# First lora products of both pairs of a batch issued together, and a new order of all steps

## The chip, the core and the metric

The kernel runs on one core of a Trainium2 chip. The metric is device time in microseconds. Before the change three runs took 446.77, 448.08 and 449.16, a median of 448.08. Within a core five queues work beside each other: TensorE (PE; its weight loads are shown as PEld), VectorE (DVE), ScalarE (ACT), GpSimd (POOL) and SyncE (SP), the last of which only issues DMAs here. Each takes its own instructions strictly in the order in which the program lists them, and waits on semaphores for the results of others.

## What is computed

The input `x` has 64 samples of 64 channels and 1024 positions. A grouped convolution (4 groups, 9 taps) with a bias per channel and a conditioning term per sample gives `v`; `v` goes through a linear layer of 1024 x 1024 with a low-rank (lora) term that is chosen per batch element by a gate, and the result is added to `x`.

```python
v   = conv1d(x, weight, groups=4, pad=4) + (cond_128 @ c_weight.T)[:, :, None] + fside[None, :, None]
A_b = sum_n gate[b, n] * lora_A[n]          # 32 x 1024
B_b = sum_n gate[b, n] * lora_B[n]          # 1024 x 32
out = x + v @ kernel + bias
        + (v @ A_b.T) @ B_b.T               # batch b: 8 samples of x
        + (v @ A_shared.T) @ B_shared.T
```

There are 8 batch elements. All is fp32; the kernel splits each operand of a large product into a high and a low part (`..hi` rounds on ScalarE, `..lo` subtracts on VectorE or GpSimd) and adds three products, high by high, high by low and low by high.

## The kernel before, in words

The 64 samples are worked in 16 **pairs** p = 0 to 15 of four samples each, and a batch element b has the two pairs 2b and 2b+1. A pair goes through these steps; the number after a step's name is the pair, then the group, quarter or product, and a last letter v, p or a says on which engine a step is put that could run on several.

- `xload p g` (L293) brings one of the four channel groups in on SP's queue. From pair 3 on, the convolution is done on sums and differences: `xdiff` (L326), `xohi`, `xolo`, `xdhi`, `xdlo` split it, `convo` (3 matmuls of 256 columns, into PSUM tile cm) and `convd` (6 of them, into cv) multiply (L346). `evmid` adds the conditioning to cm, with four activations on ScalarE (L364) or one addition on VectorE (L366); `evac` (L378) adds the two and writes `v`; `turned` (L387) transposes it into `z` on VectorE. Pairs 0 to 2 use the plain form `xhi`, `xlo`, `conv`.
- The linear layer is a 2 x 2 block product with seven products in place of eight. `asum` (L412, GpSimd) makes sums of quarters of z, `yhi` and `ylo` split the left operand, `prod p j` (L592) is product j, 12 matmuls of 512 columns. `keep` (ScalarE, L636), `xsum`, `ysum`, `radd`, `yadd` and `total` (VectorE, some on GpSimd) put the products together with the residual, which `rload` (SP) brings in; `store` (ScalarE's queue) writes the result. Pair 0 uses `plain p b k`, without the seven-product form.
- The lora term has two products. `lora p` (L602) is the first, z by A_b: 16 fp32 matmuls with 32 columns of weights, 32 records in the profile. It reads all four groups of the pair's z. Then `axlow` (ScalarE), `axsum` (VectorE), `axhi` (ScalarE) and `axlo` (VectorE) add and split its result, and `delta p b` (L660), one matmul each, adds the second product into the accumulators of quarter b. A_b and B_b come from `lload`, `mix` (TensorE, L528), `mixout`, `mixput`, `aload`, `bload`, `bhi` and `blo`.
- At the start the weights are loaded (`wload`), completed with the shared lora term (`fmm` on TensorE, `fadd` on VectorE), summed (`wsum`) and split (`whi`, `wlo`). `gmask` makes a small matrix out of the gate; `twsum`, `thi` and `tlo` prepare the convolution's weights; `cwide`, `cmul` and `csum` make the conditioning table.

What sets the order is a list: the string `ORDER` (L50 to L245) names every step once, and the program walks through it and emits each step's instructions. The instructions of each engine are then tied to each other in exactly that order, so nothing is moved by a scheduler. Tiles come from pools with fixed numbers of buffers (5 for products in PSUM, 2 for convolutions in PSUM, 4 for z, y, r and c), so that a step also waits until the tile it writes is free.

Before the change every pair had its own `lora` step at a place of its own, for instance `lora 2` between `bload 1 0` and `axlow 2` on L96 and `lora 3` on L100; `lora 0` and `lora 1` stood close together on L79.

Of the kernel before, what the change touches and what calls it, by code (L numbers as in the profile page):

```python
# [22 lines left out]
BP = NP // NB  # L23
# [27 lines left out]
small 1, warm, twload 1, busy 29, twload 0, cwload, gload, ctload, cwide, cmul, thi 2, small 0, thi 0, tlo 0 v,  # L51
xload 0 0, xhi 0 0, tlo 2 p, xload 0 1, xlo 0 0 v, conv 0 0, twsum v, xhi 0 1, xlo 0 1 v, conv 0 1, sbload 1,
sbhi 1, csum, evac 0 0 v, turned 0 0, xload 0 2, xhi 0 2, xload 0 3, saload 0, sblo 1 p, xlo 0 2 p, evac 0 1 v,
turned 0 1, saload 1, gmask, xhi 0 3, conv 0 2, xlo 0 3 p, sahi 1, conv 0 3, sahi 0, salo 0 v, fmm 0 1,
sbload 0, sbhi 0, fmm 1 1, wload 1 0, evac 0 2 a, xload 1 0, sblo 0 v, fmm 1 0, salo 1 v, xload 1 1, xhi 1 0,
xhi 1 1, xlo 1 1 p, xlo 1 0 v, turned 0 2, yhi 0 0, ylo 0 0 p, wload 0 1, fadd 0 1, evac 0 3 a, fadd 1 0,
conv 1 0, whi 7 0, fmm 4 0, turned 0 3, xload 1 2, xhi 1 2, wlo 7 0 v, fmm 3 0, wload 1 1, conv 1 1, fadd 1 1,
wload 4 0, fmm 0 0, whi 0 1, wload 0 0, fadd 0 0, evac 1 0 a, plain 0 1 0, fadd 4 0, xlo 1 2 p, turned 1 0,
whi 0 0, wlo 0 1 p, fmm 2 1, fmm 2 0, yhi 0 7, evac 1 1 a, conv 1 2, fmm 5 0, wload 2 1, wload 2 0, fadd 2 0,
wlo 0 0 p, plain 0 0 0, xload 1 3, fadd 2 1, wload 5 0, xhi 1 3, fmm 4 1, xlo 1 3 p, plain 0 0 1, whi 0 2,  # L60
ylo 0 7 v, fadd 5 0, plain 0 3 0, whi 7 1, yhi 0 4, wload 3 0, fadd 3 0, whi 0 3, wload 5 1, fmm 3 1, conv 1 3,
turned 1 1, wlo 7 1 v, wload 3 1, xload 2 0, plain 0 1 1, fadd 3 1, whi 7 2, evac 1 2 v, wlo 7 2 p, wload 4 1,
wlo 0 3 p, wlo 0 2 v, lload 0 6, plain 0 2 0, whi 7 3, plain 0 3 1, fadd 4 1, wload 7 1, turned 1 2, whi 1 1,
plain 0 1 2, lload 0 7, xhi 2 0, plain 0 0 2, ylo 0 4 v, plain 0 3 2, xlo 2 0 v, plain 0 2 1, fmm 5 1,
evac 1 3 a, xload 3 0, wlo 7 3 v, plain 0 2 2, turned 1 3, whi 1 0, yhi 0 1, ylo 0 1 v, fadd 5 1, whi 6 1,
conv 2 0, wload 7 0, thi 1, xdiff 3 0 0 v, wload 6 0, evac 2 0 a, lload 1 5, wlo 1 0 p, fmm 7 0, fadd 7 0,
plain 0 2 3, plain 0 0 3, fmm 6 0, lload 0 2, plain 0 3 3, plain 0 1 3, fadd 6 0, lload 0 5, whi 6 0, asum 1 2,
yhi 1 2, lload 0 0, yhi 1 0, plain 0 0 4, plain 0 2 4, wsum 2 2 v, whi 2 2, lload 1 1, wlo 1 1 p, plain 0 0 5,
fmm 6 1, tlo 1 v, plain 0 2 5, rload 0 2, wlo 6 0 v, wsum 2 1 v, wsum 2 3 v, whi 1 2, wlo 1 2 v, plain 0 1 4,
whi 2 1, asum 1 3, whi 1 3, wlo 1 3 p, xload 2 2, wload 6 1, fadd 6 1, xload 2 1, whi 6 2, lload 0 1, xhi 2 2,  # L70
plain 0 3 4, lload 0 4, plain 0 2 6, lload 1 0, lload 0 3, wsum 2 0 v, fmm 7 1, plain 0 2 7, xload 2 3,
plain 0 0 6, fadd 7 1, whi 6 3, total 0 2, lload 1 6, mix 0 0, mixout 0 0 a, wlo 6 2 v, xhi 2 1, wlo 6 3 v,
wlo 6 1 v, wsum 3 2 v, xlo 2 2 v, mix 0 3, mixout 0 3 a, mix 0 2, mixout 0 2 a, wsum 3 0 v, wsum 5 0 v,
mixput 0 0, whi 2 3, mix 0 1, wsum 3 1 v, mix 1 0, mixput 0 3, mixout 0 1 a, xdiff 3 0 1 p, wsum 4 0 v,
conv 2 2, wlo 2 2 v, whi 2 0, wlo 2 0 v, ylo 1 2 v, plain 0 1 5, wsum 5 1 v, rload 0 0, wsum 5 2 v, wsum 4 2 v,
xlo 2 1 v, plain 0 0 7, mixput 0 1, ylo 1 0 p, mixput 0 2, wlo 2 1 v, prod 1 0, plain 0 1 6, wsum 3 3 v,
wsum 5 3 v, rload 0 1, plain 0 3 5, wsum 4 3 v, bihi, whi 3 2, keep 1 0, plain 0 1 7, lload 1 3, wsum 4 1 v,
plain 0 3 6, mixout 1 0 a, lload 1 7, mix 1 3, aload 0, whi 5 3, yhi 1 3, rload 0 3, lload 1 2, ylo 1 3 v,
mixout 1 3 a, total 0 1, lora 0, mix 1 1, turned 2 0, lora 1, whi 5 0, bilo, xohi 3 0, lload 1 4, mix 1 2,  # L79
whi 4 2, wlo 4 2 v, mixout 1 1 a, xolo 3 0 v, whi 3 0, wlo 3 0 v, wlo 3 2 v, yhi 1 1, ylo 1 1 v, mixout 1 2 a,  # L80
asum 1 5, total 0 0, whi 4 1, conv 2 1, axlow 1, axsum 1, xload 3 2, wlo 4 1 p, wlo 2 3 v, whi 4 0,
plain 0 3 7, axlow 0, axsum 0, mixput 1 0, mixput 1 3, wlo 4 0 v, xhi 2 3, xlo 2 3 v, wlo 5 3 v, axhi 1,
prod 1 1, biput 0, axlo 1, whi 3 3, asum 1 6, yhi 1 6, wlo 3 3 v, mixput 1 1, evac 2 1 a, turned 2 1, aload 1,
mixput 1 2, total 0 3, evac 2 2 v, turned 2 2, bload 0 0, whi 3 1, axhi 0, prod 1 2, keep 1 2, conv 2 3,
bhi 0 0, biput 1, yhi 2 0, evac 2 3 a, blo 0 0 v, axlo 0, yhi 1 4, bload 0 1, wlo 3 1 p, prod 1 3, ylo 2 0 v,
delta 0 0 1, total 0 0 1, bhi 0 1, blo 0 1 v, ylo 1 6 p, prod 1 6, whi 4 3, delta 0 3 1, wlo 4 3 v, store 0 0,
ylo 1 4 p, turned 2 3, delta 0 2 1, total 0 3 1, xdhi 3 0, convo 3 0, yhi 1 5, whi 5 1, ylo 1 5 v, xdlo 3 0 v,
delta 1 0, total 0 2 1, xload 3 1, keep 1 3, prod 1 4, evmid 3 0 a, store 0 3, xohi 3 1, xdiff 3 1 0 v,
xdiff 3 1 1 p, wlo 5 1 p, delta 0 1 1, total 0 1 1, wlo 5 0 v, xolo 3 1 p, convd 3 0, evac 3 0, turned 3 0,
asum 2 3, rload 1 0, convo 3 1, yhi 2 1, xdhi 3 1, xdlo 3 1 v, prod 2 0, whi 5 2, store 0 2, delta 1 2,  # L90
xload 3 3, keep 2 0, wlo 5 2 p, yhi 2 3, prod 1 5, total 1 0, xohi 3 3, xolo 3 3 v, asum 2 2, xdiff 3 2 0 p,
store 1 0, convo 3 3, evmid 3 1 a, xdiff 3 2 1 p, convd 3 1, ylo 2 3 v, prod 2 3, rload 1 3, delta 1 1,
ylo 2 1 v, xsum 1, asum 2 5, prod 2 1, xdhi 3 2, evac 3 1, turned 3 1, rload 1 2, radd 1 2 v, xdlo 3 2 v,
xdiff 3 3 0 v, delta 1 3, xohi 3 2, xdiff 3 3 1 p, yhi 2 5, xolo 3 2 v, ylo 2 5 p, yhi 2 2, ylo 2 2 v,
evmid 3 3 a, radd 1 3 v, convo 3 2, total 1 2, store 0 1, evmid 3 2 a, convd 3 2, xdhi 3 3, xdlo 3 3 v,
rload 1 1, radd 1 1 v, bload 1 0, lora 2, axlow 2, asum 2 6, prod 2 2, total 1 1, convd 3 3, evac 3 2,  # L96
turned 3 2, axsum 2, xload 4 0, xohi 4 0, xolo 4 0 p, bhi 1 0, yhi 2 4, ylo 2 4 v, axhi 2, prod 2 5, keep 2 3,
yhi 3 0, ysum 1 p, xdiff 4 0 0 v, xdiff 4 0 1 v, prod 2 4, store 1 1, xload 4 1, xohi 4 1, xolo 4 1 p,
yadd 1 v, blo 1 0 v, xdhi 4 0, axlo 2, delta 2 0, yhi 2 6, evac 3 3, keep 2 2, xdlo 4 0 v, convo 4 0,
turned 3 3, convd 4 0, rload 2 0, evmid 4 0 a, total 1 3, total 2 0, ylo 3 0 v, lora 3, xdiff 4 1 0 v,  # L100
xdiff 4 1 1 p, asum 3 3, yhi 3 3, prod 3 0, convo 4 1, ylo 3 3 v, evac 4 0, turned 4 0, xdhi 4 1, xload 4 3,
xohi 4 3, xdlo 4 1 v, asum 3 2, xolo 4 3 v, yhi 3 2, ylo 2 6 v, xload 4 2, xdiff 4 2 0 p, store 1 2,
xdiff 4 2 1 p, xohi 4 2, prod 3 3, yhi 3 1, bload 1 1, evmid 4 1 a, delta 2 2, ylo 3 2 v, xolo 4 2 v, asum 3 5,
store 2 0, convd 4 1, xdhi 4 2, xsum 2, convo 4 2, evmid 4 2 a, evac 4 1, xdlo 4 2 v, rload 2 2, radd 2 2 p,
total 2 2, xdiff 4 3 0 v, xdiff 4 3 1 p, prod 2 6, turned 4 1, yhi 3 4, bhi 1 1, convd 4 2, evac 4 2, keep 3 0,
prod 3 2, ylo 3 1 v, rload 2 3, radd 2 3 v, ysum 2 v, convo 4 3, yadd 2 v, xdhi 4 3, xdlo 4 3 v, ylo 3 4 v,
aload 2, prod 3 1, convd 4 3, turned 4 2, blo 1 1 p, xload 5 0, yhi 3 5, xohi 5 0, keep 3 2, asum 3 6,
keep 3 3, xload 5 1, xohi 5 1, delta 2 3, prod 3 4, delta 2 1, xdiff 5 0 0 p, xdiff 5 0 1 v, axlow 3,
ylo 3 5 p, evmid 4 3 a, total 2 3, prod 3 5, store 2 3, xolo 5 0 p, rload 2 1, yhi 3 6, radd 2 1 p, rload 3 0,
axsum 3, evac 4 3, axhi 3, turned 4 3, yhi 4 0, axlo 3, delta 3 0, xload 5 2, xdhi 5 0, store 1 3, xdlo 5 0 v,  # L110
convd 5 0, convo 5 0, ylo 3 6 v, bload 2 0, ylo 4 0 v, xdiff 5 1 0 v, xdiff 5 1 1 p, total 2 1, prod 3 6,
evmid 5 0 a, prod 4 0, asum 4 3, yhi 4 3, evac 5 0, xsum 3, yhi 4 4, ylo 4 3 p, delta 3 3, delta 3 2,
total 3 0, ylo 4 4 v, lora 4, xolo 5 1 p, xdhi 5 1, xdlo 5 1 v, store 3 0, yhi 4 1, ylo 4 1 v, xohi 5 2,
convo 5 1, keep 4 0, bhi 2 0, prod 4 1, rload 3 3, asum 4 2, yhi 4 2, radd 3 3 v, turned 5 0, xdiff 5 2 0 p,
ysum 3 v, evmid 5 1 a, xdiff 5 2 1 v, ylo 4 2 v, delta 3 1, xolo 5 2 p, rload 3 1, radd 3 1 p, blo 2 0 v,
# [702 lines left out]
```

## Time and profile before

| what | before |
| --- | --- |
| median of three runs | 448.08 us |
| the execution with profile | 447.48 us |
| span of its instructions | 445.7 us |
| first lora blocks (`lora`) | 16, of which 14 stand alone |
| evictions of cm (`evmid`) on ScalarE | 52, 48.2 us of records |
| share of the span, by the chain that ended last | TensorE 91%, DMA 4%, VectorE 2% |

The page has a line of busy time for each engine, and the same in 40 slices; the chain of work that ended last; and the costliest groups of instructions. Queries of the trace give the waits by engine and releaser (time in total, times, longest), timelines of an engine (start, duration, line, operation, output and inputs) and sums of busy time by stretch of the span. A record's duration is longer than the step from one start to the next where instructions are pipelined. TensorE's clock was granted in full throughout.

### The profile page before, as it was taken

The numbers are of one execution on the slowest core, as the hardware profiler recorded it, in microseconds if no ns is written. First come the engines' busy times: TensorE is split into PE (matmuls) and PEld (weight loads), VectorE is DVE, ScalarE is ACT, GpSimd is POOL, SyncE is SP. The second block draws the span as 40 slices with busy tenths as digits, with TensorE's granted clock in tenths as the row PEclk, the third lists the DMA queues.
The fourth block names the chain that finished last, engine by engine and source line by source line (L and its number), as shares of the span: only waits on it lengthen the run. The fifth ranks groups of instructions, "written<-read, shape, count | busy, mean of one in ns | idle before, by whom it ended". The sixth has DMA issues, their size and how long they took to land.

```text
span 445.7 us, 7717 instructions
## 1 busy us (share of the span) xinstructions
PE 438.3 (98%) x2557; PEld 358.7 (80%) x2557; DVE 391.3 (88%) x615; ACT 251.2 (56%) x639; POOL 234.5 (53%) x202
## 2 busy tenths in 40 slices
PE   8999999999999999999999999999999999999996
PEld 7677658888888888888878888888888888888884
DVE  5998979899899899889899899899798989887783
ACT  5877468556655566446555655646554745654440
POOL 3766024754747653555444445464656475467543
PEclk9999999999999999999999999999999999999999
DMA  8999582461625463534345453443536354262243
GB/s 229 300 280 308 147 251 66 142 186 49 186 82 158 136 190 110 170 120 136 97 139 147 151 182 91 119 142 90 175 98 186 95 169 151 72 222 90 91 150 118
DMA packets 52488, 67.05 MB, mean 150 GB/s; under 512 B 6112, under 2 KB 34016, under 8 KB 52448
## 3 DMA queue, kind: packets, MB, share of 16 engines
q1 hardware_dynamic: 42512, 49.83, 38.9%
q10 hardware_dynamic: 9936, 16.73, 10.2%
q8 instruction: 20, 0.33, 0.3%
q14 instruction: 20, 0.16, 0.1%
HBM read 47.65 MB, written 18.87 MB: 149 GB/s over the span
## 4 chain that ended last, share of the span: by engine, by line
PE 91%; DMA 4%; DVE 2%; issue 1%; SPq 0%; ACT 0%; ACTq 0%; DVEq 0%
PE mm_a L592 19%; PE mm_d L592 18%; PE mm_c L592 17%; PE mm_b L592 9%; PE cv L346 8%; PE cm L346 4%; PE axp L602 3%; PE cv L318 2%; DMA wr<-in_dram 2%; PE mx L528 2%; PE mm_a L580 1%; PE mm_c L580 1%; DMA ls<-in_dram 1%; DMA ctt<-in_dram 1%; PE mm_d L580 1%; PE mm_a L660 1%
## 5 line engine op out<-in xcount | busy, mean ns | idle before, releaser
L592 PE MATMUL mm_a<-wh,y 128*128 128x512 f32 x240 | 79.6, 392 | 0.0
L592 PE MATMUL mm_d<-wh,y 128*128 128x512 f32 x240 | 79.2, 391 | 0.0
L592 PE MATMUL mm_c<-wh,y 128*128 128x512 f32 x240 | 79.1, 391 | 0.0
L364 ACT ACTIVATE md<-cm,cadd 128x64 f32<-128x64 f32 x208 | 48.2, 315 | 44.8 <-PE cm L346 41.1
L326 POOL TENSOR_TENSOR xf<-xt 128x256 f32<-128x256 f32 x45 | 33.3, 747 | 49.4 <-DVE xd L270 39.4
L265 ACT CAST xd<-xf 128x512 fp32r<-128x512 f32 x52 | 32.5, 626 | 44.9 <-PE cv L346 20.7
L265 ACT CAST y<-s 128x512 fp32r<-128x512 f32 x60 | 37.2, 624 | 30.5 <-POOL s L412 15.3
L592 PEld LDWEIGHTS mm_a<-wh,y 128*128 128x128 f32 x240 | 45.1, 188 | 9.9 <-issue 0.4
L592 PEld LDWEIGHTS mm_d<-wh,y 128*128 128x128 f32 x240 | 45.1, 188 | 9.2 <-issue 0.2
L592 PEld LDWEIGHTS mm_c<-wh,y 128*128 128x128 f32 x240 | 45.1, 188 | 9.1 <-ACT c L636 0.2
L387 DVE STREAM_TRANSPOSE z<-v 128x512 f32<-128x512 f32 x64 | 45.4, 709 | 3.2 <-PE axp L602 1.9
L592 PE MATMUL mm_a<-wl,y 128*128 128x512 f32 x120 | 46.9, 391 | 0.0
L592 PE MATMUL mm_c<-wl,y 128*128 128x512 f32 x120 | 46.8, 390 | 0.0
L592 PE MATMUL mm_d<-wl,y 128*128 128x512 f32 x120 | 46.8, 390 | 0.0
L346 PE MATMUL cv<-xd,th 128*128 128x256 f32 x208 | 45.7, 282 | 0.4 <-DVE xd L270 0.4
L378 DVE TENSOR_TENSOR v<-cv,md 128x512 f32<-128x512 f32 x52 | 35.7, 686 | 7.7 <-PE cv L346 2.5
L270 DVE TENSOR_TENSOR xd<-xf,xd 128x512 fp32r<-128x512 f32 x41 | 34.5, 842 | 7.6 <-ACT xd L265 7.4
L270 DVE TENSOR_TENSOR y<-s,y 128x512 fp32r<-128x512 f32 x49 | 38.2, 782 | 3.0 <-ACT y L265 2.7
L592 PE MATMUL mm_b<-wh,y 128*128 128x512 f32 x120 | 39.6, 391 | 0.0
L346 PEld LDWEIGHTS cv<-xd,th 128*128 128x128 f32 x208 | 35.5, 188 | 2.4 <-DVE xd L270 0.6
L265 ACT CAST y<-z 128x512 fp32r<-128x512 f32 x49 | 30.6, 625 | 11.8 <-DVE c L641 4.5
L326 DVE TENSOR_TENSOR xf<-xt 128x256 f32<-128x256 f32 x59 | 33.7, 587 | 0.2
(132 smaller groups left out, 1008.2 us busy)
## 6 DMA issues: line engine op xcount, KB each, us to landing
xt<-in_dram SPq DMA_DIRECT2D x64, 258.0 KB, 3.2
r<-in_dram SPq DMA_DIRECT2D x64, 256.0 KB, 3.5
out_dram<-r ACTq DMA_DIRECT2D x63, 256.0 KB, 2.6
ls<-in_dram SPq DMA_DIRECT2D x16, 256.0 KB, 4.6
br<-eff SPq DMA_DIRECT2D x48, 64.0 KB, 2.8
wr<-in_dram SPq DMA_DIRECT2D x16, 176.0 KB, 4.2
eff<-ls SPq DMA_DIRECT2D x16, 128.0 KB, 2.7
wr<-in_dram SPq DMA_DIRECT2D x16, 80.0 KB, 3.9
```

The lines of the kernel that those rows point to most:

```text
L265: nc.scalar.copy(dst, src)
L270: engs[eng].tensor_tensor(dst, src, f32(hi), ALU.subtract)
L318: nc.tensor.matmul(ps, a[:, 2 * kt, g, :], b[:, :, kt:kt + P], start=(n == 0), stop=(n == 5))
L326: engs[eng].tensor_tensor(xdf[p, g][:, e], m, odd(p, g), ALU.subtract)
L346: nc.tensor.matmul(ps, a[:, w, g, :], b, start=(n == 0), stop=(n == 2))
L364: nc.scalar.activation(t[:, n], cpm[p, g][:, n], ACTF.Identity, bias=c[:, n:n + 1])
L378: nc.vector.tensor_tensor(v.rearrange("p n (i e) -> p e n i", e=2), cps.pop((p, g)), mid.pop((p, g)).unsqueeze(1).to_broadcast([P, 2, 4, H ...
L387: nc.vector.transpose(z[:, :, :, :, gg, :], vs.pop((p, g)).rearrange("p m j -> p (m j)"))
L528: nc.tensor.matmul(mps[w, j][n * e:n * e + n], gm.rearrange("p b i -> p (b i)"), lraw[w, 2 * j + e], start=True, stop=True)
L580: nc.tensor.matmul(acc[p, BLOCKS[b]], m[:, kk, :], n, start=(k == 0 and q == 0), stop=(k == 7 and q == 2))
L592: nc.tensor.matmul(ps, a[:, k, :], b[bb, k], start=s, stop=(k == HK - 1 and q == 2), skip_group_check=not first)
L602: nc.tensor.matmul(axp[q * R:q * R + R, p % 2, :], a[:, k, :], zs[p, hf][:, k, :], start=k < 2, stop=k >= 6)
```

## The change

A new step `loras b` issues the first lora products of both pairs of a batch, one behind the other. It takes the place of the single `lora` steps for batches 1 to 7; batch 0 keeps `lora 0` and `lora 1`. The whole string `ORDER` is replaced by another order of the same steps, from the first line to the last, with new choices of engine for many of them. No step's code is altered.

```diff
+    def loras(b):
+        for p in range(BP * b, BP * b + BP):
+            lora(p)
```

The start of the list, which is typical of the rest:

```diff
-small 1, warm, twload 1, busy 29, twload 0, cwload, gload, ctload, cwide, cmul, thi 2, small 0, thi 0, tlo 0 v,
-xload 0 0, xhi 0 0, tlo 2 p, xload 0 1, xlo 0 0 v, conv 0 0, twsum v, xhi 0 1, xlo 0 1 v, conv 0 1, sbload 1,
+cwload, warm, busy 29, twload 1, gload, gmask, ctload, twload 0, twsum v, xload 0 0, cwide, saload 0, thi 2,
+xload 0 1, thi 0, tlo 2 v, small 0, tlo 0 p, xhi 0 0, xlo 0 0 v, sahi 0, salo 0 v, sbload 0, xhi 0 1,
+xlo 0 1 v, sbhi 0, sbload 1, sbhi 1, cmul, sblo 0 v, csum, conv 0 0, evac 0 0 v, turned 0 0, xload 0 3,
...
-rload 1 1, radd 1 1 v, bload 1 0, lora 2, axlow 2, asum 2 6, prod 2 2, total 1 1, convd 3 3, evac 3 2,
-turned 3 3, convd 4 0, rload 2 0, evmid 4 0 a, total 1 3, total 2 0, ylo 3 0 v, lora 3, xdiff 4 1 0 v,
...
+ylo 2 5 v, yhi 3 0, xdhi 4 0, ylo 3 0 v, xdlo 4 0 v, loras 1, rload 1 3, radd 1 3 v, yhi 2 6, convo 4 0,
...
+prod 15 0, keep 15 0, evac 15 3, turned 15 3, loras 7, yhi 15 4, rload 14 2, prod 14 6, radd 14 2 p, ysum 14 p,
...
+prod 15 4, delta 15 1, rload 15 2, total 15 0, store 15 0, radd 15 2 p, delta 15 2, total 15 2, store 15 2,
+prod 15 6, rload 15 1, radd 15 1 v, totalh 15 1 1, storeh 15 1 1, totalh 15 1 0, storeh 15 1 0
```

How the steps with a choice of engine are placed before and after, where the numbers differ by two or more (the rest moves by one, or trades places pair by pair):

| step | before | after |
| --- | --- | --- |
| `evmid` | ScalarE 52 | ScalarE 36, VectorE 16 |
| `blo` | VectorE 10, GpSimd 6 | VectorE 13, GpSimd 3 |
| `xdlo` | VectorE 41, GpSimd 11 | VectorE 38, GpSimd 14 |
| `xlo` | VectorE 7, GpSimd 5 | VectorE 10, GpSimd 2 |
| `xolo` | VectorE 30, GpSimd 22 | VectorE 28, GpSimd 24 |
| `wlo` | VectorE 21, GpSimd 11 | VectorE 23, GpSimd 9 |
| `wsum` | VectorE 16 | VectorE 14, GpSimd 2 |
| `radd` | VectorE 36, GpSimd 9 | VectorE 38, GpSimd 7 |
| `ysum` | VectorE 13, GpSimd 2 | VectorE 11, GpSimd 4 |

On TensorE the mixes are placed differently too: before, `mix 0 0`, `0 3`, `0 2`, `0 1` and `1 0` stand in one row; after, `mix 0 0` and `mix 0 2` each stand alone between `plain` steps, and `mix 0 3`, `1 0`, `0 1` and `1 2` stand in one row.

## The prediction, made before the changed kernel ran

> **What bounds the kernel now.** The views were read in this order: the page's busy time, the waits of TensorE, the sums by stretch, then TensorE's and VectorE's timelines. One execution with profile took 447.48 us, of which 445.7 are the span; the median of the three runs shown is 448.08, 0.6 above it. Sums below are made against the 447.48 and 0.6 is added at the end.
>
> ```profile
> PE 438.3 (98%) x2557; PEld 358.7 (80%) x2557; DVE 391.3 (88%) x615; ACT 251.2 (56%) x639; POOL 234.5 (53%) x202
> ```
>
> TensorE is busy all but 7.4 us. Of its waits, all that the view names come to 3.2 us, and those that are not the warm-up or a `conv` of the first pairs are these:
>
> ```profile
> PE cv L346 <- DVE xd L270: 0.4, 1, 0.4
> PE mx L528 <- DMA ls<-in_dram: 0.4, 1, 0.4
> ```
>
> So the total is TensorE's list of work plus what it loses early. The sums by stretch (busy us and counts of PE, PEld, DVE, ACT, POOL; clock; DMA share) tell who is next:
>
> ```profile
> 20.00:45.00 25.00, 25.00 (x108) 19.33 (x108) 23.71 (x37) 17.87 (x40) 16.73 (x13) 1.00 0.95 293
> 45.00:70.00 25.00, 24.55 (x157) 15.04 (x154) 21.91 (x39) 15.97 (x35) 4.27 (x3) 1.00 0.65 180
> 70.00:100.00 30.00, 29.99 (x172) 24.86 (x171) 26.96 (x39) 18.62 (x51) 18.14 (x15) 1.00 0.47 144
> 100.00:130.00 30.00, 30.00 (x180) 25.40 (x179) 28.25 (x46) 17.12 (x46) 17.84 (x17) 1.00 0.33 99
> ```
>
> The reader is to see that VectorE is at 88 to 95% beside TensorE from 20 to 130 us, ScalarE and GpSimd are far below, and the DMA engines are nearly full until 45. VectorE is the engine that can become the bound.
>
> **The lora blocks.** A lora block is 32 matmul records (16 matmuls in two passes) with weights of 32 columns. Its edges on TensorE's timeline (start, duration):
>
> ```profile
> 140.41 0.40 PE L660 MATMUL mm_b<-bst,axt 98*128 98x512 f32 x1
> 140.65 0.39 PE L660 MATMUL mm_c<-bst,axt 98*128 98x512 f32 x1
> 140.97 1.08 PE L602 MATMUL axp<-z,ar 128*32 128x128 f32 x32
> 141.98 0.39 PE L346 MATMUL cm<-xo,th 128*128 128x256 f32 x1
> 142.21 0.28 PE L346 MATMUL cm<-xo,tl 128*128 128x256 f32 x1
> 142.32 0.28 PE L346 MATMUL cm<-xo,th 128*128 128x256 f32 x1
> ```
>
> From start to start, a 512-wide matmul takes 0.23 to 0.24 but the last one before the block takes 0.32: 0.09 to get in. The block takes 1.01. The first 256-wide matmul after it takes 0.23 where the next takes 0.11: 0.11 to get out. All 14 blocks of pairs 2 to 15 show the same 0.09 and 0.11 within 0.01, so an edge pair costs **0.20**. Merging two blocks removes one exit and one entry; the seam inside is a step like those within the block, 0.03 on average. Seven merges: 7 x 0.20 = 1.4 off. Against it, the new order puts `mix 0 0` and `mix 0 2` alone between `plain` steps, where before five mixes stood together; a mix block shows 0.32 on entry too, and I take 0.20 each: 0.4 on. Net **-1.0**. Ends: 0 (if the seam costs what the edges cost) and -1.4.
>
> Here the Trainium skill speaks against the change. "TensorE: Matmul & The Clock Gate", section "Step-by-step: what each phase is for", says weight loads are pulled ahead of matmuls in flight, so the next tile's weights load while this one runs. By that rule a block's edge costs nothing and the merge is worth 0. In the trace the first weight load of the block starts only with the block, at 140.97, after 0.36 us idle. I take the row: -1.0, not 0.
>
> **VectorE's running sum.** The order is one list of steps, and each engine takes its own in that order. So for each TensorE step I add what VectorE has in its queue up to the result that this step needs, and compare it with TensorE's own sum up to there. Records of VectorE overlap, so I use start-to-start steps:
>
> ```profile
> 6.21 0.68 DVE L270 TENSOR_TENSOR tl<-tw,th 128x512 fp32r<-128x512 f32 x1
> ...
> 6.81 0.69 DVE L270 TENSOR_TENSOR xsl<-xt,xsh 128x516 fp32r<-128x516 f32 x1
> ...
> 8.62 0.41 DVE L736 TENSOR_TENSOR cadd<-pc,fst 128x256 f32<-128x256 f32 x1
> ```
>
> 0.60 is such a step when undisturbed; means over the execution (some steps take 1.3) are: z 0.65, v 0.67, y 0.74, xd 0.76, r<-r,c 0.69, xo 0.57, xf 0.49, wl 0.65, wr 0.60 to 0.64, sums out of PSUM 0.61. TensorE: product 2.745, plain 0.68, conv 1.42, convd 0.71, convo 0.355, delta 0.235, mix 0.45, lora 1.21. VectorE starts at 4.8 (`cwide`), TensorE's real work is set at 7.4, the first `conv`.
>
> Before, the worst place is `conv 2 3`, which needs the PSUM tile that `evac 2 2` frees. TensorE: 7.4 + 11 conv 15.6 + 32 plain 21.8 + 16 fmm 3.8 + 8 mix 3.6 + 3 products 8.2 + 2 lora 2.4 + cmul 0.9 = 63.8. VectorE: 4.8 + 62.2 for 97 steps = 67.0. TensorE must lose **3.2** there, whatever happens. From 75 us on VectorE is ahead (by 1.3 at 82, 5.9 at 123, 9 at 145), and this is why no wait is left later.
>
> After, the worst place is `convo 3 2`, behind `evac 3 1`: TensorE 7.4 + 75.1 = 82.5; VectorE 4.8 + 82.4 (127 steps) = 87.2, a deficit of **4.7**. It is 3.7 at 120 (`delta 2 3` behind `blo 1 1`), 1.4 at 123, 0.9 still at 167 (`prod 5 5` behind `ylo 5 5`), and VectorE is ahead only from 180 on. Two causes. Up to `evac 3 1` it has six more steps (121 before: 3 more xlo, 2 more wlo, 2 more ylo, ...) while two products fewer stand ahead on TensorE. And 16 `evmid` move from ScalarE to VectorE: on ScalarE four activations each, 48.2 / 52 = 0.93; on VectorE nearest is the row of cadd above, same size and also out of PSUM, 0.41 recorded, 0.36 a step: 16 x 0.36 = 5.8 more on VectorE, 2.2 of it (six) before 167; where VectorE is ahead it costs 0. With all other moves between v, p and a its whole sum grows by about 7 (388 to 395). ScalarE's relief and GpSimd's nearly equal load (238 to 236) are worth nothing, since nobody waits for them for long.
>
> The start is part of this sum, not added to it: `gmask` (1.25) and `twsum` (0.61) now stand ahead of `cwide`, so the first `conv` moves from 7.5 to about 9.3. `gmask` waits for gg, second of ScalarE's DMAs instead of third, so not later than `cwide` waited before. Before, TensorE lost 0.78 and 0.54 to xsl soon after; those are absorbed. Loads: weights that `fadd` needs land by my count of bytes (0.28 MB/us) up to 3 us behind TensorE's new order at 20 us, but VectorE gets to those fadd 3 to 4 us later still, so it hides them. Later moves of xload, rload, store and bload past each other on SP: before, SP blocks up to 10 us on a store and nobody waits; cost 0, at most 1 to 2 if an xload is caught behind a late store. A new wait: `loras` needs the z tiles of both pairs, and all four z buffers are held until then; the next `turned` on VectorE is queued at least one product later, so 0. If that cover went, evac, xdiff and with them `convd` would stand behind it.
>
> The end: `prod 15 5` needs `ylo 15 5`, now on GpSimd behind `radd 14 2` 1.35, `ysum 14` 1.34, two `asum` 1.5 each, plus `yhi` 0.62 and itself 1.38: 7.7 after `turned 15 3`, which itself ends 1 to 1.5 after `convd 15 3`. TensorE has `prod 15 0`, `loras 7`, `prod 14 6` and up to four deltas before it, 2.7 + 2.2 + 2.7 + 0.9 = 8.5. I take 0, at most 1. `rload 15 1` and `radd 15 1` stand behind the last product in the list, but nothing on SP holds the load back: 0, at most one radd, 0.7.
>
> **Sum.** Edges -1.0. Deficit 4.7 instead of 3.2: +1.5. While VectorE sets the pace, its own short waits (for ScalarE mostly) count: it idled 3.0 of 70:100, of which I take a third, +1.0. The one mid-run loss before, 0.6 at 233, need not come back: -0.6. Together +0.9: 448.4 in that execution's terms, **449.0** against the median.
>
> **Rivals.**
> Slower: VectorE stays the pace far beyond 87 us. Its idle time of before then counts in full: to 123, 3.7 + 3.0 + 1.4 - 3.2 = 4.9, less 1.0, is +3.9, **452.0**; to 168, 0.9 + 8.0 - 3.2 - 1.0 = +4.7, 452.8. It decides once VectorE's idle time between 67 and 123 is over 3. For it: almost no lead until 167. Against: before, much of that idle time was VectorE waiting for TensorE, which falls away.
> Faster: VectorE's backlog removes its waits. Before it lost 1.9 near 57 us, a `turned` waiting for a `lora` that waited for its DMA; here VectorE gets there later. -1.0 + 1.5 - 1.9 - 0.9 = -2.3, **445.8**. Against: it asks for everything at once.
> No effect of the merge itself: +1.9, 450.0; against it are the equal 0.09 and 0.11 of 14 blocks.
>
> **How the numbers follow.** Likeliest case 0.50 (447 to 450.3, no-effect included), slower rival 0.39, faster 0.11. About 0.5%, or 2.2 us, is what a measurement of this kernel can tell from no change. So faster 0.11, same 0.50, slower 0.39. The range 446 to 453.5 leaves out the faster rival's tail and the slower one's.
>
> **What would show it.** 7 blocks of 64 records with one entry of 0.09 and one exit of 0.11; cm evictions of about 0.41 on VectorE; VectorE at 95% or more from 20 to 120; TensorE waits on VectorE between 20 and 110, none after 180. Wrong if TensorE waits after 180, or if waits on DMA or GpSimd carry the loss.

## The result, and the profile after

The change made the kernel slower: 459.83 us (459.67 to 460.67, 4 runs) against 448.30 (446.77 to 449.16, 4 runs), a ratio of **1.0265** with a 95% interval of 1.0234 to 1.0296. The forecast was 449.0 with a range up to 453.5: the measured time lies 6.3 us above its upper end. The profiled execution took 460.67, with a span of 458.8 against 445.7.

The page of the changed kernel, its busy time, the granted clock in 40 slices and the chain that ended last, and below it the chain of the kernel before:

```profile
PE 445.5 (97%) x2557; PEld 361.1 (79%) x2557; DVE 403.1 (88%) x633; ACT 236.5 (52%) x574; POOL 236.8 (52%) x201
...
PEclk9999999999899999999999999999999999999999
...
PE 75%; DVE 10%; DMA 6%; issue 3%; ACT 2%; SPq 1%; POOL 1%; DVEq 0%; ACTq 0%; POOLq 0%
```
```profile
PE 91%; DMA 4%; DVE 2%; issue 1%; SPq 0%; ACT 0%; ACTq 0%; DVEq 0%
```

Three things are to be seen. TensorE is busy for 7.2 us more than before although it does the same 2557 instructions. One slice of the clock, near 115 us, is an 8. And TensorE's part of the chain went from 91% to 75%, VectorE's from 2% to 10%.

What TensorE waited for (in total, times, longest):

```profile
PE cm L345 <- DVE v L377: 2.3, 1, 2.3
PE idle L704 <- DVE axt L698: 1.2, 1, 1.2
PE pf L474 <- POOL sa L269: 1.1, 1, 1.1
PE pf L474 <- POOL sb L269: 1.0, 1, 1.0
PE mm_a L663 <- DVE axt L626: 1.0, 1, 1.0
PE cv L345 <- DVE xd L269: 0.9, 1, 0.9
PE cm L345 <- DVE xo L269: 0.6, 1, 0.6
```

The second is the warm-up, which was there before. The pf lines are two `fmm` of the start, which wait from 12 and from 19 us on. The other four are new, and each is a single long wait: `delta 2 0` and `convo 4 2` near 112 us, `convo 8 2` at 230, `convd 10 3` at 291. The sums by stretch, in the columns used before:

```profile
20.00:45.00 25.00, 24.67 (x103) 18.67 (x104) 23.50 (x38) 17.40 (x41) 13.32 (x9) 1.00 0.98 303
45.00:70.00 25.00, 25.00 (x161) 15.48 (x160) 23.19 (x38) 15.62 (x37) 6.68 (x6) 1.00 0.61 167
70.00:100.00 30.00, 30.00 (x147) 24.99 (x146) 27.36 (x42) 19.34 (x50) 16.38 (x15) 1.00 0.45 142
100.00:130.00 30.00, 28.46 (x185) 22.92 (x184) 27.52 (x48) 13.64 (x35) 11.29 (x10) 0.94 0.43 132
```

From 45 to 100 us TensorE has no gap. In the last row it idles for 1.54 us, and its clock is 0.94 there. How the halved clock looks, on TensorE's timeline of that place (start, duration):

```profile
111.68 0.40 PE L591 MATMUL mm_b<-wh,y 128*128 128x512 f32 x1
113.05 0.47 PE L663 MATMUL mm_a<-bst,axt 98*128 98x512 f32 x1 [0.98 <-DVE axt L626]
113.51 0.36 PE L345 MATMUL cm<-xo,th 128*128 128x256 f32 x1
113.70 0.28 PE L345 MATMUL cm<-xo,tl 128*128 128x256 f32 x1
114.54 0.64 PE L345 MATMUL cm<-xo,th 128*128 128x256 f32 x2 [0.56 <-DVE xo L269]
114.98 0.41 PE L345 MATMUL cm<-xo,tl 128*128 128x256 f32 x1
115.19 0.41 PE L345 MATMUL cm<-xo,th 128*128 128x256 f32 x1
115.41 0.63 PE L591 MATMUL mm_a<-wh,y 128*128 128x512 f32 x1
115.83 0.63 PE L591 MATMUL mm_a<-wl,y 128*128 128x512 f32 x1
```

The 256-wide steps take 0.21 instead of 0.12 and the 512-wide ones 0.42 instead of 0.23. The clock's own record has 0.5 for 3.41 us from 114.74 on. In 3.4 us at such steps, 3.4 x (1 - 0.234 / 0.42) = 1.5 us of TensorE's work is lost in this execution, on top of the waits that stand right before (from start to start, 1.15 and 0.72 above a normal step). In time it is less. Of the four executions two had a mean granted clock of 0.996 (460.67 and 459.89 us) and two of 1.000, with no such stretch (459.67 and 459.77): 0.1 to 1.0 us apart. Why the rest of the 1.5 does not show was not tried.

To add up the loss, each step of TensorE (the time from one instruction's start to the next one's) was set against a normal one for its shape (512 columns 227 ns, 256 columns 117, a record of a lora block 31.6). The normal steps sum to some 425 us in every kernel here. What is above them, in us by stretch, with the two kernels of the experiments that matter most beside it (`a_lay` is the changed order at the old addresses, `a_fix4` the same with its lists mended):

```
stretch (us)   before   after   a_lay   a_fix4
  0 -  40        5.6     8.0     7.9     7.9
 40 - 100        2.9     2.0     1.4     1.4
100 - 140        0.5     4.7     3.2     3.6
140 - 220        1.5     2.3     1.1     1.3
220 - 300        2.0     6.1     6.8     2.5
300 - end        2.5     4.8     1.9     1.8
sum             15.0    27.9    22.2    18.5
```

The column of after is higher even from 300 us on, where TensorE has only one wait of 0.4. There every product is a little slower: its 512-wide step is 234.1 ns on average (1263 steps, the few over 300 left out) where it was 228.4, the same in every stretch of 40 us. 1263 x 5.7 ns is **7.2 us**, the largest single part of the loss, and nothing in the diff seemed to touch it.

### The profile page after: what moved, and what is told of

Same layout as the page of the kernel before. It is cut to its first block, busy times and chain, and to the rows that moved or that the text cites. A ratio compares the mean times of both kernels' runs of the same rounds, so it can differ in the third digit from the quotient of the medians.

```text
span 458.8 us, 7648 instructions
## 1 busy us (share of the span) xinstructions
PE 445.5 (97%) x2557; PEld 361.1 (79%) x2557; DVE 403.1 (88%) x633; ACT 236.5 (52%) x574; POOL 236.8 (52%) x201
## 4 chain that ended last, share of the span: by engine, by line
PE 75%; DVE 10%; DMA 6%; issue 3%; ACT 2%; SPq 1%; POOL 1%; DVEq 0%; ACTq 0%; POOLq 0%
PE mm_d L591 16%; PE mm_c L591 16%; PE mm_a L591 14%; PE mm_b L591 8%; PE cv L345 7%; PE cm L345 3%; PE axp L601 2%; DMA wr<-in_dram 2%; DVE y L269 2%; PE mx L527 1%; DVE r L669 1%; DMA xt<-in_dram 1%; DVE xd L269 1%; DMA sbr<-in_dram 1%; DVE r L652 1%
## 5 line engine op out<-in xcount | busy, mean ns | idle before, releaser
L591 PE MATMUL mm_a<-wh,y 128*128 128x512 f32 x240 | 81.5, 401 | 0.0
L591 PE MATMUL mm_d<-wh,y 128*128 128x512 f32 x240 | 80.5, 397 | 0.0
L591 PE MATMUL mm_c<-wh,y 128*128 128x512 f32 x240 | 80.4, 396 | 0.0
L363 ACT ACTIVATE md<-cm,cadd 128x64 f32<-128x64 f32 x144 | 33.2, 316 | 41.0 <-PE cm L345 36.5
L591 PE MATMUL mm_a<-wl,y 128*128 128x512 f32 x120 | 48.1, 401 | 0.0
L269 DVE TENSOR_TENSOR y<-z,y 128x512 fp32r<-128x512 f32 x42 | 36.3, 869 | 1.7 <-ACT y L264 1.6
L269 DVE TENSOR_TENSOR xd<-xf,xd 128x512 fp32r<-128x512 f32 x38 | 31.2, 822 | 6.2 <-ACT xd L264 6.2
L269 POOL TENSOR_TENSOR xd<-xf,xd 128x512 fp32r<-128x512 f32 x14 | 20.4, 1456 | 30.9 <-ACT xd L264 30.9
```

The lines of the kernel that those rows point to most:

```text
L269: engs[eng].tensor_tensor(dst, src, f32(hi), ALU.subtract)
L363: nc.scalar.activation(t[:, n], cpm[p, g][:, n], ACTF.Identity, bias=c[:, n:n + 1])
L591: nc.tensor.matmul(ps, a[:, k, :], b[bb, k], start=s, stop=(k == HK - 1 and q == 2), skip_group_check=not first)
```

## The experiments

The theories at first: **layout**, that new addresses of tiles in SBUF make the matmuls slower; **order**, that the new lists do (VectorE's load, other engines' traffic). Each kernel below was timed beside the kernel before on the same chip, and its ratio to that is given with a 95% interval.

### Is it the addresses?

The pool gives places in the order in which kinds of tiles are first named. Before, `xhi 0 0` and `xhi 0 1` claimed the places of xo and xd, and then `sbload 1` the 57 weight pieces. After, `saload 0` comes ahead of both. Addresses stand in no trace. Read off the compiled kernels, the pieces start at byte 69440 of a partition before and at 61152 after, the y tiles at 204608 in both; the 8288 bytes between are the size of the two xo tiles (2080 each) and the xd tile (4128) that changed places with the pieces. Two kernels moved the pieces by 32 bytes, the changed one (`a_align`) and the one before (`b_shift`), with the same edit:

```diff
     def piece(name, shape=(P, HN), dtype=F32):
-        return work.tile(list(shape), dtype, tag="w", name=name, bufs=57)
+        if not pads:
+            pads.append(work.tile([P, 8], F32, tag="pa", name="pa", bufs=1))
+        t = work.tile(list(shape), dtype, tag="w", name=name, bufs=57)
+        if len(pads) < 2:
+            pads.append(work.tile([P, 8], F32, tag="pb", name="pb", bufs=1))
+        return t
+    pads = []
```

> The changed kernel with two unused 32-byte tiles, one ahead of the 57 weight pieces in SBUF and one behind them, so that the pieces begin at a multiple of 64 bytes as they did before (the change's new first step to claim a piece, a load of the shared lora, had put them 32 bytes beside it), and all other tiles keep their place within 64 bytes. Theory LAYOUT: the 512-wide matmuls that stream a weight piece take 234 ns a step after and 227 before (means 234.4 and 228.7) because of the 32 bytes; about 1347 of them x 5.7 ns = 7.7, so 459.8 - 7.7 = 452.1 us, and the median step is 227 again. Rival ORDER: the longer step comes from the new order (queues, semaphores, what VectorE and GpSimd do at the same time), so 459.8 us and a step of 234.

> The kernel before with the same two 32-byte tiles, which here put its weight pieces 32 bytes beside a multiple of 64; its order is untouched. Theory LAYOUT: 448.3 + 7.7 = 456.0 us, median step of the products 234. Rival ORDER: 448.3 us, step 227.

`a_align` took 457.99 (1.0194, 1.0169 to 1.0219) with a mean step of 232.5; `b_shift` 454.15 (1.0119, 1.0094 to 1.0144) with 233.0. Its order untouched, the kernel before lost 5.3 us to unused bytes: layout matters. But `a_align` did not get its step back, so alignment to 64 bytes isn't the rule. The next two kernels exchanged the whole layout:

```diff
# a_lay: the changed kernel, places of xo and xd claimed first
     def piece(name, shape=(P, HN), dtype=F32):
+        if not room:
+            for n in range(2):
+                room.append(work.tile([P, 4, JB], F32R, tag="xo", name=f"room{n}", bufs=2))
+            room.append(work.tile([P, 2, 4, JB], F32R, tag="xd", name="room2", bufs=1))
# b_lay: the kernel before, a step "room" ahead of xhi 0 0
+    def room():
+        for n in range(57):
+            piece(f"room{n}")
```

> The changed kernel with every tile at the SBUF address that it had before (the places of xo and xd are claimed ahead of the first weight piece); order untouched. Shifting by 32 bytes both ways moved the mean step of a product's matmul between four values, one for each layout (228.4 before, 233.0 shifted; 234.1 after, 232.5 aligned to 64), so it is the layout but not the 64 bytes alone. Theory LAYOUT: the mean step is 228.4, 1263 x (234.1 - 228.4) = 7.2 less, 459.8 - 7.2 = 452.6 us, or some 2 less where the clock is not halved. Rival CONTENTION (the engines' traffic of the new order makes the step longer and the address only shifts it a little): step 231 or more, 456 us or more.

> The kernel before with every tile at the address that it has in the changed kernel; order untouched. Theory LAYOUT: mean step 234.1, 1261 x 5.7 ns = 7.2 more, 455.5 us. Rival CONTENTION: 228.4 to 231, at most 451.5.

`a_lay`: step 228.4, 455.29 us (1.0153, 1.0133 to 1.0173). `b_lay`: step 234.1, 455.02 (1.0137, 1.0120 to 1.0154). The steps are exactly the forecast ones. The groups by line show the same thing in the recorded duration (busy us, mean ns). Before, then after, `a_lay` and `b_lay`:

```profile
L592 PE MATMUL mm_a<-wh,y 128*128 128x512 f32 x240 | 79.6, 392 | 0.0
```
```profile
L591 PE MATMUL mm_a<-wh,y 128*128 128x512 f32 x240 | 81.5, 401 | 0.0
```
```profile
L597 PE MATMUL mm_a<-wh,y 128*128 128x512 f32 x240 | 79.4, 391 | 0.0
```
```profile
L594 PE MATMUL mm_a<-wh,y 128*128 128x512 f32 x240 | 80.9, 398 | 0.0
```

The same order is slower or quicker by its addresses alone. In time it is 4.5 us (459.83 to 455.29) on the changed kernel and 6.6 (448.44 to 455.02) on the one before, less than 7.2 on the first; that TensorE's waits take up part of it where VectorE sets the pace fits, but was not tried by itself. Rival contention fell: with the new order and all its traffic the step is 228.4.

What of the addresses is it? Five more kernels are the one before with other sums of unused bytes ahead of the pieces, each run once (`[P, 8]` above becomes another size, and the tile behind fills up to 256):

> The kernel before with its weight pieces 64 bytes further (64 and 192 unused bytes ahead of them and behind them), all others in place within 256 bytes. A look at the step alone. If it depends on the piece's start within 128 bytes (64 of 128: 228.4; 0: 232.5; 32 or 96: 233 to 234), it is 232.5 here. If it is 64 bytes that count and the rest came from the other tiles, it is 228.4.

> As b_w64, with the pieces 128 bytes further. If the start within 128 bytes counts, the mean step is 228.4 again; if it is the distance between the piece and the y tile (0 of 256 before), it is higher, 232 to 233.

> The kernel before with its weight pieces 32 bytes further and all other tiles in place within 256 bytes: a piece starts 32 bytes (of 256) behind a y tile. If the distance of the two operands sets the step, this is a value of its own, between those at 0 (228.4) and 64 (229.7) or above both; if 32 of 64 bytes is what costs, 233 to 234.

> As b_d32 at a distance of 96. By distance: between 64 (229.7) and 128 (232.5), near 231; by 32 of 64 bytes: 233 to 234.

> As b_d32 at a distance of 192, the pieces at a multiple of 2048. By distance: between 160 (234.1) and 224 (233.0), near 233.5; by the piece's own start: 0 of 256 should be at least as good as 64 of 256, 228.4 or less.

All layouts, by the distance from a y tile (the weights of the matmul) to a weight piece (what it streams), within 256 bytes:

```
distance   mean step (ns), kernels               piece's own start
   0       228.4  before, a_lay and its repairs       64
  32       233.2  b_d32                               96
  64       229.7  b_w64                              128
  96       233.5  b_d96                              160
 128       232.5  a_align; 232.6 b_w128             0; 192
 160       234.1  after, b_lay                       224
 192       233.2  b_d192                               0
 224       233.0  b_shift                             96
```

The one pair with equal distance and different starts, `a_align` and `b_w128`, has the same mean and the same distribution of steps (most at 228 to 233, a fifth at 236 to 241). The pair with the same start 0, `a_align` and `b_d192`, has different ones (in `b_d192` most are at 231 to 237). So the step goes with the distance of the two operands and not with the piece's own start, as far as these two pairs tell. It doesn't grow with the distance: my 231 for 96 was a miss, 0 is best, 64 costs 1.3 ns, all others 4 to 6. Tiles that moved along with y (z, v, xf) aren't told apart from it; but the matmul reads only these two. The single times of the five (452.40 to 456.76 us) are all above the median of before.

### What is a merge worth?

The edges of a merged block, on the timeline of the changed kernel (x64 is the whole block):

```profile
216.67 0.28 PE L345 MATMUL cm<-xo,tl 128*128 128x256 f32 x1
216.79 0.27 PE L345 MATMUL cm<-xo,th 128*128 128x256 f32 x1
216.99 1.95 PE L601 MATMUL axp<-z,ar 128*32 128x128 f32 x64
218.88 0.39 PE L345 MATMUL cv<-xd,th 128*128 128x256 f32 x1
219.10 0.28 PE L345 MATMUL cv<-xd,tl 128*128 128x256 f32 x1
```

In: 0.20 where 0.12 is normal, so 0.09 (unrounded). Out: 0.22 instead of 0.12, so 0.11. The block itself takes 1.89, where two of 32 take 2.02: of the 0.20 from a block's last record to the next start, only 0.07 remains at the seam. So a merge takes away 0.20 + 0.13 = 0.33, seven take **2.3**. Three kernels tried it against the time. `b_loras` is the kernel before with six merges, each put where the later pair's lora stood (batch 3: between the two), `a_split` undoes the merges of `a_align`, and `a_fix_split` those of `a_fix` (below) in another way:

```diff
# b_loras, batch 4
-..., lora 8, ..., axlow 8, ..., axsum 8, axhi 8, ..., lora 9
+..., loras 4, axlow 8, axsum 8, axhi 8, axlo 8
# a_split, batch 7
-loras 7, yhi 15 4, rload 14 2, prod 14 6, ..., axlow 14
+lora 14, yhi 15 4, rload 14 2, prod 14 6, lora 15, ..., axlow 14
# a_fix_split, batch 7
-prod 15 0, ..., loras 7
+prod 15 0 0 3, lora 14, prod 15 0 3 1, ..., lora 15
```

> The kernel before with six of the seven merges (batches 1, 2, 3, 4, 6, 7; each lora and its followers moved to where both pairs' z tiles are ready) and nothing else of the change; layout as before. Theory EDGES: 6 x 0.20 = 1.2 off, 447.1 us. Rival RULE (weight loads are pulled ahead, an edge is worth 0): 448.3 us. If the moved deltas make TensorE wait, the waits show behind the moved delta steps and are to be taken out of the sum.

> The changed kernel with its weight pieces aligned as in a_align, and each loras block split again: the second pair's lora one product or convolution later, all else in place. Theory EDGES: 7 x 0.20 = 1.4 us more than a_align, with 14 blocks of 32 records that show 0.09 in and 0.11 out. Rival RULE: the same time as a_align.

> a_fix with each loras block split again, now without a later result: the first pair's lora goes 3 matmuls (or one small step) earlier, the second's stays at the end of the old block, so nothing that reads them waits longer. Theory EDGES: 7 x 0.20 = 1.4 us more than a_fix. Rival RULE (weight loads are pulled ahead): the same time as a_fix.

`b_loras` took 473.79 us (1.0552, 1.0522 to 1.0581) and `a_split` 469.09 (1.0439, 1.0415 to 1.0463): both say nothing of edges, since both made a `delta` wait. Why, in `a_split`, first TensorE and then ScalarE:

```profile
439.51 1.08 PE L606 MATMUL axp<-z,ar 128*32 128x128 f32 x32
442.82 0.77 PE L668 MATMUL mm_c<-bst,axt 98*128 98x512 f32 x1 [2.24 <-DVE axt L631]
```
```profile
440.65 0.52 ACT L617 COPY axq<-axp 32x128 f32<-32x128 f32 x2 [3.93 <-PE axp L606]
```

The copy is pair 14's `axlow`, and pair 14's block ended at 436.6. It starts only when pair 15's block, the one in the first line, is over: the two pairs' results lie in one PSUM tile, and here the reader of one half waited for the last writer of either. Then ScalarE, VectorE, ScalarE and VectorE follow, and `delta 14 2` is 2.2 us late. Four stretches of halved clock stand behind waits of `a_split`. In `b_loras` the waits on `axlo` were 4.8, those on the eviction of cm 4.7.

`a_fix_split` delays no result. It took 456.81 (1.0164, 1.0120 to 1.0207) and `a_fix` 452.79, 4.0 less. This difference is no measure of the edges: the two intervals overlap, and the times go with the clock. The one run of `a_fix_split` at a granted clock of 1.00 took 452.25, its five at 0.991 to 0.995 took 456.19 to 458.78; `a_fix` took 451.27 to 453.25 at 0.996 to 0.998, and 457.05 and 457.00 at 0.991 and 0.993. What the edges cost is read from the records. The 14 blocks of 32 in `a_fix_split` show them again, which refutes that they cost nothing; and behind 140 us, where six of the seven merges are, TensorE's steps lose 2.2 us more than in `a_fix`, against 6 x 0.33 = 2.0. Near 117 us the halved clock of the profiled execution lasted 6.83 us instead of 3.41, another 1.5. The forecast 1.4 was too little; by the records it is 2.3.

### The lists

`a_lay` still lost 6.9 us against before. VectorE's timeline of the changed kernel ahead of the long wait at 230 us:

```profile
225.87 0.69 DVE L269 TENSOR_TENSOR y<-z,y 128x512 fp32r<-128x512 f32 x1
226.48 0.68 DVE L269 TENSOR_TENSOR y<-s,y 128x512 fp32r<-128x512 f32 x1
227.08 1.52 DVE L269 TENSOR_TENSOR xo<-xt,xo 128x256 fp32r<-128x256 f32 x1
228.52 1.78 DVE L652 TENSOR_TENSOR r<-r,c 128x512 f32<-128x512 f32 x1
230.23 0.68 DVE L669 TENSOR_TENSOR r<-mm_a,r 128x512 f32<-128x512 f32 x1
230.83 0.57 DVE L618 TENSOR_TENSOR axs<-axp,axq 32x128 f32<-32x128 f32 x2
231.43 0.69 DVE L377 TENSOR_TENSOR v<-cv,md 128x512 f32<-128x512 f32 x1
```

The last line is `evac 8 1`, which frees the PSUM tile for `convo 8 2`. TensorE was through with the `convd` ahead of that at 229.8. VectorE had stood idle for 0.36 us until 220.6, waiting for ScalarE's copy out of the lora block, and then had 10.8 us of steps in its list up to `evac 8 1`, with a `radd` of 1.78 among them that nobody needed yet.

That `radd` shows something else too. A `r<-r,c` step takes 0.68 in the 19 cases in which GpSimd is idle all the while, and 1.10 on average, up to 1.83, in the 27 in which GpSimd works for half of it or more; `v<-cv,md`, which reads one operand from PSUM, takes 0.69 in both. GpSimd worked from 226.96 to 229.75, under the xo of 1.52 (0.41 alone) and under this `radd`: 2.2 us of stretching ahead of a wait of 2.46. Ahead of the waits at 112 and 291 it is the same: an axt of 1.39 (0.42 alone), and two y of 1.77 and 1.78 (0.68 alone). Over an execution, what such steps take above their time alone comes to some 45 us before and 49 after, so their places changed more than their sum. A kernel without GpSimd's steps at these places was not run; how much of the waits is the list's order and how much the stretching stays open.

`a_fix` is `a_lay` with such steps moved by a few places around the three long waits:

```diff
# at 226 us
-ylo 7 1 v, ylo 7 3 v, asum 7 5, xolo 8 2 v, radd 6 3 v, prod 7 1, total 6 0, axlow 7, axsum 7, evac 8 1, axhi 7, turned 8 1
+ylo 7 1 v, evac 8 1, xolo 8 2 v, ylo 7 3 v, asum 7 5, prod 7 1, total 6 0, axlow 7, axsum 7, axhi 7, radd 6 3 v, turned 8 1
# at 289 us
-ylo 9 4 v, ..., turned 10 2, xdhi 10 3, prod 9 1, xdlo 10 3 v, convd 10 3
+xdhi 10 3, prod 9 1, xdlo 10 3 v, turned 10 2, ylo 9 4 v, convd 10 3
# at 111 us: total 1 3, evmid 4 0, axlo 2, xolo 4 2 earlier; xdiff 4 1, xdhi 4 1, convo 4 2 later
```

> a_lay (the changed kernel at the addresses of before) with twelve steps moved by a few places around its three mid-run stalls, on VectorE's list and TensorE's: total 1 3, evmid 4 0, axlo 2 and xolo 4 2 earlier, xdiff 4 1 and convo 4 2 later (the stall of 1.43 + 0.72 at 111 us); evac 8 1 and xolo 8 2 ahead of radd 6 3 (2.51 at 226); turned 10 2 and ylo 9 4 behind xdlo 10 3 (1.12 at 289). Theory LOCAL LISTS (TensorE waits because the needed VectorE step stands behind others that could wait, while VectorE as a whole has time): the stalls go, 5.8, and with them the halved clock that follows the longest one, 1.7: 455.3 - 7.5 = 447.8 us. Rival VECTORE IS THE BOUND (what is taken from one place comes back later): the stalls move, 453 us or more.

452.79 us (1.0110, 1.0059 to 1.0161), not 447.8. At 226 and 289 the waits are gone and did not come back: 220 to 300 us loses 2.5 in the mended kernels, where `a_lay` lost 6.8, 3.6 of it in these two waits and some in a halved clock behind the first. At 111 it was a miss. The wait moved:

```profile
PE mm_c L595 <- DVE r L673: 2.3, 1, 2.3
...
PE cv L343 <- ACT md L361: 0.9, 1, 0.9
```

The first is `prod 3 3`, waiting for an accumulator that `total 2 0` empties. `total 2 0` waited for its residual, and SyncE's queue shows when that was asked for:

```profile
114.14 0.37 SPq L290 DMA_DIRECT2D xt<-in_dram  x1
114.60 1.19 SPq L639 DMA_DIRECT2D r<-in_dram  x2
```

`xload 5 0` stands ahead of `rload 2 0` in the list and waits for a buffer that `xdiff 4 1` frees, which I had moved back; the load behind it, for a tile long free, left at 114.6. Three more kernels went on from there: `a_fixs` (also `sblo 1` and `salo 1` on VectorE), `a_fix2` (the stores ahead, `fmm 4 1` behind `conv 1 1`) and `a_fix4` (the stretch laid out anew):

```diff
# a_fixs
-sblo 1 p ... salo 1 p
+sblo 1 v ... salo 1 v
# a_fix2, on top of a_fix
-axsum 2, total 1 3 ... xdhi 4 1, store 1 2 ... evmid 4 1 a ... store 1 3 ... rload 2 0
+axsum 2, total 1 3, store 1 2, store 1 3, rload 2 0 ... convo 4 1, evmid 4 1 a, xdhi 4 1
-fmm 4 1 ... fadd 4 1 ... conv 1 1
+conv 1 1, fmm 4 1, fadd 4 1
# a_fix4, from loras 1 on
+loras 1, rload 1 3, axlow 2, axsum 2, axhi 2, radd 1 3 v, ..., yadd 1 v, rload 2 0, ..., axlo 2, xohi 4 1, total 1 3, blo 1 0 v,
+evmid 4 0 v, xolo 4 1 v, ..., prod 2 5, delta 2 0, ..., rload 2 2, xload 5 0, ..., convo 4 1, ..., prod 3 0, total 2 0, xsum 2, convo 4 2
# a_fix5, on top of a_fix4: delta 4 2, delta 4 0 behind convo 6 2, delta 8 0 behind prod 8 6
```

> a_fix with sblo 1 and salo 1 on VectorE instead of GpSimd, for which TensorE waits 0.89 and 1.25 at 11 and 18 us. Theory START: these two go, VectorE gets 1.2 more in a stretch in which it has little room: 1 to 2 us less than a_fix. Rival: VectorE is late with the next xlo instead, 0 to 1.2 us more than a_fix.

> a_fix with six more steps moved. In a_fix the wait at 111 us was gone, but 1.05 and 2.48 stood at 115 and 117: xdhi 4 1, put later, held up ScalarE's queue, with store 1 2, store 1 3 and evmid 4 1 behind it, so rload 2 0 got its place late, total 2 0 was late, and prod 3 3 waited for the accumulator. Here both stores stand right behind total 1 3, rload 2 0 behind them, evmid 4 1 ahead of xdhi 4 1; and fmm 4 1 with fadd 4 1 stands behind conv 1 1 (1.25 at 18 us). Theory LOCAL LISTS: 1.05 + 2.48 + 1.7 (the halved clock) + 1.25 = 6.5 less than a_fix (452.8), 446.3 us, under the kernel before. Rival VECTORE IS THE BOUND: 452 us or more, with the waits elsewhere.

> a_lay with the moves of a_fix at 226 and 289 us, the start left as the change has it, and the stretch from loras 1 to convd 4 1 laid out anew: axsum 2, axhi 2 and axlo 2 come ahead of what can wait, rload 2 0 ahead of xload 5 0 (which held up SP's queue until 114 us in a_fix, because it waits for a buffer that xdiff 4 1 frees), prod 3 0 ahead of convo 4 2. Theory LOCAL LISTS: the 3.5 us lost there in a_fix and the halved clock of 1.7 go: 452.8 - 5.2 = 447.6 us. Rival VECTORE IS THE BOUND around 111 us: 3 us of waits stand somewhere between 105 and 125 once more, and 451 to 452 us.

> a_fix4 with delta 4 2 and delta 4 0 behind convo 6 2 and delta 8 0 behind prod 8 6, where TensorE waits 0.5 each for axlo. LOCAL LISTS: 0.8 less than a_fix4, about 446.8 us, under the kernel before by a little. Rival: the same as a_fix4, as their totals come later.

- `a_fixs`: 455.24 (1.0149, 1.0103 to 1.0194). A miss; `fmm 1 1` now waits 2.7 for VectorE instead of 0.5 for GpSimd. VectorE has no room at the start.
- `a_fix2`: 452.00 (1.0068, 1.0044 to 1.0092), not 446.3. Between 110 and 119 us it waits 1.3, 1.0 and 0.6, now because the stores hold up ScalarE, which VectorE's `xolo 4 1` needs; its clock stayed at 1. At the start the wait only went to `conv 0 2` and `conv 1 0`.
- `a_fix4`: 451.32 (1.0066, 1.0052 to 1.0080), where 447.6 or 451 to 452 was expected: the rival is right for this place. VectorE works without a gap from 104 to 120 us and TensorE still waits, at 115 us for VectorE (the second line) and at 123 us for a `keep` on ScalarE (the first):

```profile
PE mm_a L595 <- ACT c L643: 1.3, 1, 1.3
...
PE cv L343 <- DVE xd L267: 1.2, 1, 1.2
```

- `a_fix5`: 451.43 (1.0086, 1.0062 to 1.0110), the same as `a_fix4`, where 446.8 was expected; the small waits grew at the next step instead. None of these kernels beats the one before.

What is left of `a_fix4`'s 3 us is in the table above: 2.3 at the start and 3.1 between 100 and 140 us; the other stretches are 1.9 better than before, the merges' 2.3 among it.

## Why the prediction was wrong

**Its largest omission: a term for the layout.** It counted instructions and queues, and gave each matmul its old duration. The new order names the weight pieces ahead of two other kinds of tiles, and their distance to y went from 0 to 160 within 256 bytes: 5.7 ns on each of 1263 steps. Undone alone it gives 4.5 us back; alone it costs the kernel before 6.6. Without it the result would have been 455.3, still above the range.

**The step that failed in the argument: "VectorE is ahead only from 180 on", and "none after 180".** Two of the four new waits stand at 230 and 291 us, together 3.5. The running sum let VectorE carry a lead forward, with one average cost for each kind of step. But VectorE's list holds results of TensorE (`total`, `axsum`, `keep`'s followers), so each lead ends where it must wait for one: it waited until 220.6 and owed 10.8 us of steps nine microseconds later, 2.2 of them the stretching beside GpSimd, whose load the prediction had put at nothing. `a_fix` shows it from the other side; the same work in another local order has no such wait.

**Its deficits came from a wrong size.** `mix` stands in TensorE's sum with 0.45. The five mixes that stand in one row in the kernel before take 0.93 each:

```profile
44.17 4.67 PE mx L528 x20
```

Both sums contain 8 mixes, so TensorE's side is 3.9 us too short in both. Put right, VectorE's deficit is none before (67.0 against 67.7 us), 0.8 instead of 4.7 at `convo 3 2`, and none at 120 us, where the prediction had 3.7. The place named for the kernel before was wrong as well: `conv 2 3` started at 71.5 us, ahead of the `evac 2 2` that was to free its tile (72.4). So the waits forecast between 20 and 110 us did not come: 45 to 100 has no gap, `convo 3 2` began without a wait, and VectorE was at 91 to 94% and not at 95. That TensorE did lose 1.9 us in waits at 111 to 114, near the 120 of the sum, was luck: the sum done rightly has no deficit there. `a_fix`, `a_fix2` and `a_fix4` moved these waits and could not remove them; why not is open. Of the rivals the slower one had the direction, and neither the price nor the reason.

**The halved clock was not in the sum.** It was taken as 1.00, as before. Behind waits of 1.9 us TensorE lost another 1.5 in the profiled execution; in the four times it is at most 1.0.

**The edges were mis-sized.** 0.09 and 0.11 were read rightly and came out the same; the 0.13 that the end of a block saves at the seam was left out ("0.03 on average"). A merge is worth 0.33, seven 2.3 and not 1.4. The rule that weight loads are pulled ahead, against which I took the row, would have made it 0; the Trainium skill ("TensorE: Matmul & The Clock Gate", "Step-by-step: what each phase is for") states it under two conditions, which the prediction left out. Of lone mix blocks there is one more than before (five against four), not two.

**The start.** The first `conv` came at 8.2 and not at 9.3, and `cmul` waited for `cwide` as thought. "The start is part of this sum, not added to it" was wrong: two `fmm` wait 1.0 and 1.1 for `sblo 1` and `salo 1` on GpSimd, which I had not looked at, and the first 40 us lose 2.4 more.

**Right:** the 16 additions of `evmid` on VectorE took 0.415 each (0.41 forecast), though VectorE's whole busy time grew by 11.8 and not by 7; the old wait at `convd 8 3` did not return; `loras` waited for no z tile; the end cost 0.4, at the `prod 15 5` that was named (the view names VectorE's r as its releaser, which ended at 436.45; `ylo 15 5` on GpSimd ended at 436.51, so either may have been the last); no wait of TensorE in the second half is on a DMA.

## What to carry to other kernels

When the order of first use of tiles changes, compare the addresses of the two operands of the hot matmul before and after, and a row of its steps: a change of order can slow work that it does not touch. A running sum per engine finds where an engine is short of time, but each cost in it is to be set against a row of the trace, and it must be set back to zero wherever that engine waits for a result of the other; after each such place, count what stands ahead of the next step that is needed, and see what GpSimd does meanwhile. And behind a wait of two microseconds TensorE may run at half its clock for a while.

## What the runs showed of the hardware that was not expected

- The mean step of a 512-wide fp32r matmul in a long row was 228.4 ns to 234.1 ns by the distance of its two operands in SBUF, the same in every stretch, and on other chips where a distance was met again. The 256-wide steps of convd, whose own distances were not tabulated, showed none of it (118 ns before and after).
- The clock halves after short waits, in steps of a grid: the full clock held for 109.23, 51.2, 51.2 and 215.04 us between the halved stretches of `a_split`, that is 32, 15, 15 and 63 times 3.413. The Trainium skill ("TensorE: Matmul & The Clock Gate", "What's actually happening") gives 3413 ns as a window that runs freely, and this agrees. Its table asks for at least one idle window before the clock is halved; here a whole one was not needed: waits of 1.15 and 0.72 in one window halved the clock after it, while one of 2.48 in `a_align` at 226.5, which lay across two windows (1.6 and 0.9), did not. Whether a wait is followed by a halved clock should then depend on where the grid falls in an execution. The changed kernel agrees, with a clock of 0.996 in two executions and of 1.000 in the other two; that was not tried by itself.
- A queue that only issues transfers can carry a wait across engines: a load for a free buffer left at 114.6 us because the one ahead of it waited for VectorE.
- VectorE's steps with both operands in SBUF were stretched while GpSimd worked (`r<-r,c` from 0.68 to 1.10 us on average, `y<-z,y` from 0.68 to 1.20); those that read PSUM were not (`v<-cv,md` 0.69 in both).
